# The first image's 3x3 convolution by transformed tiles of two rows by four columns

## The chip, the core and the metric

The kernel runs on one core of a Trainium2 chip. The metric is the device time of one execution in microseconds (us), given as the median of a few runs. TensorE (PE in the profile) multiplies matrices and loads its weights in a second stream (PEld); VectorE (DVE), ScalarE (ACT) and GpSimd (POOL) work elementwise; SyncE (SP) only issues DMAs. Each engine has its own instruction queue and works through it in order; semaphores connect them.

## What is computed

Two images of 256 channels and 64x64 pixels go through two layers, each of them a group normalisation, a block and a residual sum. Layer 0 is attention over all 4096 pixels with eight heads. Layer 1 has two branches. The attention branch works twice on blocks of 64 pixels; the convolution branch makes 576 channels from the same q, k and v and runs a grouped 3x3 convolution over them:

```python
x = x + _L0_conv_ref(_gn(x), ...)
x = x + _L1_conv_ref(_gn(x), ...)

# in layer 1
q, k, v = (_c1x1(x, w, b) for the three weights)
ctx = _sa(blockify(fq), blockify(fk), blockify(v), oh, ow)         # attention over a grid
feats = ...(_bn_relu(_c1x1(ctx, lr_W_w), ...))
ctx2 = _sa(qx, kx, vx, DH, DW)                                     # attention in a block
out_att = ...(_bn_relu(_c1x1(ctx2, sr_W_w), ...))
f_all = jnp.einsum('bidn,oi->bodn', jnp.concatenate([qh, kh, vh], 1), fc_w)
out_conv = lax.conv_general_dilated(f_conv, dep_w, (1, 1), ((1, 1), (1, 1)),
                                    feature_group_count=hd, ...)
return rate1 * out_att + rate2 * out_conv
```

All of it is float32. The kernel multiplies the 1x1 weights into the grouped weights, so that the convolution branch is one dense 3x3 convolution from 256 channels of the normalised x to 256 channels, plus a bias that differs at the image's edges.

## The kernel before

An image is cut into eight tiles of 512 pixels (8 rows), with the channels in two halves of 128 partitions. The images follow one another, and for each come four stages: `project0` (q, k and v of layer 0), `attention0`, `layer1_first` (the grid attention, which leaves `feats`) and `layer1_second` (the block attention and the convolution, tile by tile, and the output). While the first image ends, the generator `following()` fetches the second image's x, takes its statistics and normalises it; `step()` in the last two tiles of `layer1_second` moves it on.

In one tile t of `layer1_second`, TensorE makes the hidden and final q and k (`branch`), then in `group_attention` the values (`pvs`), the scores (`sp`), the transposes (`at`) and the context (`pc`); VectorE does the softmax between scores and transposes, and copies the transposed blocks (`bd`). The convolution is cut into steps, one step at each of up to three `spots` of a tile: spot 0 between the q and the k branch, spot 1 behind the scores, spot 2 behind the context.

The convolution is done on transformed tiles. The first image uses tiles of two rows by two columns (`conv_transform`, `conv_step`): the image falls into four strips of 16 rows, and each strip has four steps, one for each column term, 16 in all. The second image uses tiles of two rows by four columns (`wide_transform`, `wide_step`): two strips of 32 rows, six column terms, 12 steps. A step of either kind has 16 products, each of 128 by 128 by 256, and each of these is two instructions in float32. So a step has 32 matmuls. It consists of

- the transform of the normalised image `xp`: GpSimd takes a difference or sum of columns (`col`); in the wide kind VectorE adds a second term, one instruction per channel half (L1158), and a third (L1161); then GpSimd makes the four row terms `v`. `conv` asks for the transform of the next step before the products of this one;
- the products into one PSUM tile `mm`, of which there is only one, so that the next step's products wait until all of it has been read;
- a copy by ScalarE and four additions by VectorE that read `mm` and leave two output rows `z`;
- additions of `z` into the x tiles. In the wide kind z counts for up to four column phases with factors `BY`: 16 instructions of 128x256 for the column terms 1 to 4, four for the terms 0 and 5 (L1212).

The weights of the first image are made by `conv_weights` on VectorE, written to memory as 16 blocks, fetched by `fetch_conv_weights` (L1013), transposed by TensorE (L1022), scaled, and written back to `wf_kept`. The second image's `WideWeights` has four places in on-chip memory for its six sets. It fetches four of them, makes one new set (number 4) into `wf_more` and one in place (number 3) with GpSimd in `widen`, and exchanges sets between steps as `NEXT` says. The wide kind needs the image's columns apart by phase, so in the second image the x tiles are copied into that order by VectorE at the end of `layer1_first` (L1488).

The order on the engines comes from a planner that works with estimated costs, except inside `tc.manual_schedule`, where the named engines keep the order of the program. In `layer1_second` that is TensorE always, and VectorE too for the second image and for the last two tiles of the first. `tc.issue_after(i)` queues what is in it behind instruction i on that instruction's engine. Buffers: x tiles and some results share nine (`xpool`), short-lived tiles share twelve (`w4`), a transform's `col` has one. When a convolution's strip is complete, `give` adds the x tile to the attention's result and writes it out, which frees the x tile for the second image's load. `conv_edges` adds the edge terms on ScalarE.

Of the kernel before, what the change touches and what calls it, by code (L numbers as in the profile page):

```python
# [10 lines left out]
F32 = mybir.dt.float32  # L11
# [3 lines left out]
ALU = mybir.AluOpType  # L15
# [26 lines left out]
def direct_layers(ctx: ExitStack, tc: tile.TileContext, a: dict, out: bass.AP, bad: bass.AP):  # L42
# [966 lines left out]
    def fetch_conv_weights(b):  # L1009

        wf = vpool.tile([P, KC, UW, C], F32, tag="vw", name=f"wf_{b}")
        for r in range(4):
            nc.sync.dma_start(out=wf[:, :, 4 * r : 4 * r + 4, :], in_=wf_kept[:, :, 4 * r : 4 * r + 4, :])  # L1013
        if b > 0:
            return wf
        for pos in range(UW):
            r, q = divmod(pos, 4)
            pw = bank([P, KC, C], f"pw_{pos}")
            for k in range(KC):
                for m in range(2):  # L1020
                    block = slice(m * P, (m + 1) * P)
                    nc.tensor.transpose(pw[:, k, block], wf[:, k, pos, block], ident)  # L1022
            scale = (0.5 if r in (1, 2) else 1.0) * (0.5 if q in (1, 2) else 1.0)
            if pos % 2:
                nc.scalar.activation(wf[:, :, pos, :], pw, AF.Copy, scale=scale)
            else:
                nc.vector.tensor_scalar(wf[:, :, pos, :], pw, scale, None, ALU.mult)
        nc.sync.dma_start(out=wf_kept, in_=wf)
        return wf

# [3 lines left out]
    def conv_transform(b, xp, s, q):  # L1037

        def cols(d):
            return xp[:, :, 16 * s : 16 * s + 18, d : d + W - 1 : 2]  # L1040

        def rows(d):
            return col[:, :, d : d + 15 : 2, :]

        terms = ((0, 2, False), (1, 2, True), (2, 1, False), (1, 3, False))
        col = cpool.tile([P, KC, 18, W // 2], F32, tag="col", name=f"col_{b}_{s}_{q}")
        one, two, plus = terms[q]
        (nc.gpsimd.tensor_add if plus else nc.gpsimd.tensor_sub)(col, cols(one), cols(two))
        v = [w4([P, 2, KC, STRIP], f"v_{b}_{s}_{q}_{n}") for n in range(2)]
        for r, (one, two, plus) in enumerate(terms):  # L1050
            dst = v[r // 2][:, r % 2].rearrange("p k (i j) -> p k i j", j=W // 2)
            (nc.gpsimd.tensor_add if plus else nc.gpsimd.tensor_sub)(dst, rows(one), rows(two))  # L1052
        return v

    def conv_step(b, xts, wf, v, s, q, pacc, behind_products=None):


        mm = pacc.tile([P, 2, 4, STRIP], F32, tag="acc", name=f"mm_{b}_{s}_{q}")
        for r in range(4):
            for m in range(2):  # L1060
                for k in range(KC):
                    nc.tensor.matmul(  # L1062
                        mm[:, m, r, :], wf[:, k, 4 * r + q, m * P : (m + 1) * P], v[r // 2][:, r % 2, k, :],
                        start=k == 0, stop=k == KC - 1,
                    )
        if behind_products:
            behind_products()
        z = w4([P, 2, 2, STRIP], f"z_{b}_{s}_{q}")
        nc.scalar.copy(z[:, 1], mm[:, :, 1, :])
        nc.vector.tensor_add(z[:, 0], z[:, 1], mm[:, :, 0, :])  # L1070
        nc.vector.tensor_add(z[:, 0], z[:, 0], mm[:, :, 2, :])
        nc.vector.tensor_sub(z[:, 1], z[:, 1], mm[:, :, 2, :])
        nc.vector.tensor_sub(z[:, 1], z[:, 1], mm[:, :, 3, :])  # L1073
        yield
        bias = kept["bias"][1]
        for half in range(2):
            xs = xts[2 * s + half].rearrange("p m (i r j c) -> p m i r j c", i=4, r=2, c=2)
            for r in range(2):
                zs = z[:, r, :, half * (STRIP // 2) : (half + 1) * (STRIP // 2)].rearrange(
                    "p m (i j) -> p m i j", i=4  # L1080
                )
                for c in range(2):
                    dst = xs[:, :, :, r, :, c]
                    if q - c == 0:
                        for m in range(2):
                            nc.vector.scalar_tensor_tensor(  # L1086
                                dst[:, m], zs[:, m], bias[:, m, 0:1], dst[:, m], ALU.add, ALU.add
                            )
                    elif (q, c) in ((1, 0), (2, 0)):
                        nc.vector.tensor_add(dst, dst, zs)  # L1090
                    elif (q, c) in ((2, 1), (3, 1)):
                        nc.vector.tensor_sub(dst, dst, zs)

    NQ, NC, WIDE = 6, 4, W // 4
    wf_more = dram.tile([P, KC, 4, C], F32, name="wf_more")

    class WideWeights:

        TURNS = [(0, q) for q in range(NQ)] + [(1, q) for q in reversed(range(NQ))]
        NEXT = {(0, 0): 4, (0, 1): 5, (1, 5): 1, (1, 4): 0}  # L1100

        def __init__(self, b):
            self.wf = vpool.tile([P, 4, KC, 4, C], F32, tag="vw", name=f"wf_{b}")
            for q in (0, 5, 1, 2):
                self.fetch(q, 3 if q == 5 else q)

        def of(self, q):
            return self.wf[:, q % 4]

        def fetch(self, q, place):  # L1110
            for k in range(KC):
                if q == 4:
                    src = wf_more[:, k]
                else:
                    src = wf_kept[:, k].rearrange("p (r q) c -> p r q c", q=4)[:, :, min(q, 3), :]
                nc.sync.dma_start(out=self.wf[:, place, k], in_=src)

        def widen(self, r):

            stage = w4([P, 2, T], f"wide_{r}")  # L1120
            fourth, tmp = (stage[:, n, :].rearrange("p (k c) -> p k c", k=KC) for n in range(2))
            w = [self.wf[:, q, :, r, :] for q in range(4)]
            nc.gpsimd.tensor_sub(tmp, w[1], w[2])
            nc.gpsimd.tensor_scalar(tmp, tmp, 2.0, None, ALU.mult)
            nc.gpsimd.tensor_scalar(w[3], w[3], 4.0, None, ALU.mult)
            nc.gpsimd.tensor_add(w[3], w[3], w[0])
            nc.gpsimd.tensor_sub(fourth, w[3], tmp)
            nc.gpsimd.tensor_add(w[3], w[3], tmp)
            nc.sync.dma_start(out=wf_more[:, :, r, :], in_=fourth)

        def used(self, s, q):
            if (s, q) in self.NEXT:
                new = self.NEXT[s, q]
                self.fetch(new, new % 4)
# [7 lines left out]
    def wide_transform(b, xp, s, q):  # L1142
# [18 lines left out]
        nc.vector.tensor_add(col, col, cols(fourth))  # L1161
# [207 lines left out]
    def layer1_first(b, put, check, st, groups):  # L1369
# [79 lines left out]
        with tc.manual_schedule(engines={E.PE}):  # L1449

            before = None
            for t in range(NT + 1):
# [28 lines left out]
                if b and 2 <= t < 6:  # L1481
                    kept["wide"].widen(t - 2)
                if b and t:
                    new = xpool.tile([P, KC, T], F32, tag="x", name=f"xphase_{t - 1}")
                    old = st.xts[t - 1].rearrange("p k (a j c) -> p k a c j", j=WIDE, c=NC)
                    with tc.issue_after(kept["bd"].ins):
# [833 lines left out]
```

## Time and profile before

| | us |
|---|---|
| median of three runs | 2995.36 (2994.68 to 2996.34) |
| the profiled execution | 2997.0 |
| its span, first to last instruction | 2995.2 |
| TensorE, VectorE, ScalarE, GpSimd busy | 2942.2, 2497.5, 2337.2, 848.9 |
| first image, convolution products | 1307.2 to 1514.5, 512 matmuls |
| second image, convolution products | 2749.4 to 2962, 384 matmuls |

The profile is of one execution. A row of a timeline gives the start, the length, the engine, the line, the operation with output and inputs, and how many instructions are merged in it; in brackets stands the idle time before it and what ended that. A row of a table of windows gives the stretch and its length, then busy time and instructions of TensorE, its weight loads, VectorE, ScalarE and GpSimd, then the granted TensorE clock, the DMA engines' share and GB/s. Tile names show which stage an instruction belongs to: `lr` is `layer1_first`, `sr` is `layer1_second`.

### The profile page before, as it was taken

What the parts mean: (1) busy time and instruction counts of PE and PEld (TensorE: products, weight loads), DVE (VectorE), ACT (ScalarE), POOL (GpSimd) and SP (SyncE); (2) the same over time, 40 slices, a digit from 0 to 9 for tenths busy, and PEclk for the clock granted to TensorE, in tenths of its full rate; (3) what the DMA queues carried; (4) which work ended last, traced back from release to release, by engine and by line L of the source; (5) the groups of instructions that cost most, each with busy time, mean ns of one, the idle gap of its engine ahead of it and who ended that gap; (6) DMA issues with size and microseconds to landing.
All of it is one profiled execution on the core that took longest, in us unless ns stands there. A gap on an engine that the chain in (4) does not pass through costs nothing. (4 is left out here: it accounts for less than half of the span.)

```text
span 2995.2 us, 63912 instructions
## 1 busy us (share of the span) xinstructions
PE 2942.2 (98%) x25043; PEld 1826.5 (61%) x25043; DVE 2497.5 (83%) x3180; ACT 2337.2 (78%) x3283; POOL 848.9 (28%) x934
## 2 busy tenths in 40 slices
PE   7999999999999999999999999999999999999998
PEld 4555556665555556667765565566665555567665
DVE  4598998999899999966655989989998989965874
ACT  2699999999999995543236999999999999954433
POOL 1032222332232222055500222223222222262430
PEclk9999999999999999999999999999999999999999
DMA  7979778897888771131159797788978877730010
GB/s 259 274 142 181 145 162 166 161 184 149 166 178 161 149 166 51 57 138 44 59 178 264 146 180 149 163 165 162 186 147 169 176 157 153 154 91 28 8 57 30
DMA packets 254339, 430.76 MB, mean 144 GB/s; under 512 B 99352, under 2 KB 118604, under 8 KB 251852
## 3 DMA queue, kind: packets, MB, share of 16 engines
q0 software_dynamic: 96960, 237.57, 41.4%
q1 hardware_dynamic: 156924, 188.76, 23.3%
q8 instruction: 198, 3.24, 0.5%
q14 instruction: 113, 0.93, 0.1%
q10 hardware_dynamic: 144, 0.26, 0.0%
HBM read 124.27 MB, written 69.44 MB: 65 GB/s over the span
## 5 line engine op out<-in xcount | busy, mean ns | idle before, releaser
L600 ACT ACTIVATE es<-ring 128x512 f32<-128x512 f32 (+2 forms) x1574 | 1201.7, 904 | 37.6 <-PE ring L594 23.3
L594 PE MATMUL ring<-q,k 128*128 128x512 f32 x4096 | 1085.5, 407 | 7.8 <-ACT es L600 5.7
L646 DVE TENSOR_TENSOR e<-e,es 128x1024 f32<-128x1024 f32 (+1 forms) x942 | 1029.7, 1155 | 29.6 <-ACT es L600 28.1
L594 PEld LDWEIGHTS ring<-q,k 128*128 128x128 f32 x4096 | 730.9, 188 | 384.6 <-ACT es L600 117.5
L600 ACT ACTIVATE v<-ring 128x512 f32<-128x512 f32 (+2 forms) x1036 | 784.9, 891 | 17.2 <-PE ring L594 8.8
L609 PE MATMUL av<-es,v 128*32 128x256 f32 (+1 forms) x9648 | 722.6, 389 | 0.0
L646 DVE TENSOR_TENSOR e<-e,v 128x1024 f32<-128x1024 f32 (+1 forms) x624 | 669.3, 1130 | 16.8 <-ACT v L600 16.0
L609 PE MATMUL av<-v 128*32 128x256 f32 x6224 | 506.0, 389 | 0.0
L609 PEld LDWEIGHTS av<-es,v 128*32 128x32 f32 x9648 | 325.1, 109 | 263.9 <-issue 105.0
L609 PEld LDWEIGHTS av<-v 128*32 128x32 f32 x6224 | 222.2, 109 | 170.3 <-issue 70.8
L656 POOL DMA_DIRECT2D es<-es x116 | 99.0, 853 | 436.5 <-ACT es L600 406.5
L656 POOL DMA_DIRECT2D acc<-es x126 | 126.2, 1007 | 129.8 <-ACT es L600 38.8
L654 POOL DMA_DIRECT2D es<-es x20 | 11.4, 568 | 492.4 <-ACT es L600 263.3
L656 POOL DMA_DIRECT2D es<-v x74 | 63.3, 855 | 292.1 <-ACT v L600 256.5
L656 POOL DMA_DIRECT2D v<-es x114 | 115.8, 1016 | 24.7 <-ACT es L600 9.3
L1062 PE MATMUL mm<-v,wf 128*128 128x256 f32 x512 | 113.6, 380 | 0.9 <-DVE z L1073 0.9
L656 POOL DMA_DIRECT2D acc<-v x86 | 88.8, 1032 | 88.7 <-DMA acc<-es 36.6
L1062 PEld LDWEIGHTS mm<-v,wf 128*128 128x128 f32 x512 | 96.4, 190 | 16.1 <-issue 3.4
L1052 POOL TENSOR_TENSOR v<-col 128x512 f32<-128x512 f32 x64 | 83.0, 1325 | 74.2 <-DVE x L1086 23.1
L1166 POOL TENSOR_TENSOR v<-col 128x512 f32<-128x512 f32 x48 | 60.5, 1290 | 113.3 <-DVE col L1161 105.3
L1181 PE MATMUL mm<-v,wf 128*128 128x256 f32 x384 | 85.6, 381 | 0.0
L984 DVE SCALAR_TENSOR_TENSOR prep<-prep 128x256 f32<-128x256 f32 x198 | 83.7, 478 | 0.4
(283 smaller groups left out, 2818.7 us busy)
## 6 DMA issues: line engine op xcount, KB each, us to landing
acc<-es POOLq DMA_DIRECT2D x122, 512.0 KB, 6.2
acc<-v POOLq DMA_DIRECT2D x78, 512.0 KB, 6.2
es<-es POOLq DMA_DIRECT2D x136, 256.0 KB, 4.1
v<-es POOLq DMA_DIRECT2D x134, 256.0 KB, 5.2
k<-wk_halves SPq DMA_DIRECT2D x64, 512.0 KB
q<-wq_halves SPq DMA_DIRECT2D x256, 128.0 KB
v<-v POOLq DMA_DIRECT2D x88, 256.0 KB, 4.9
es<-v POOLq DMA_DIRECT2D x86, 256.0 KB, 4.2
```

The lines of the kernel that those rows point to most:

```text
L594: touch(nc.tensor.matmul(sc[:, i, :], held["k", g // 2][:, j * P : (j + 1) * P], held["q", g, u // 2][:, u % 2, :], start=True, stop=True, ...
L600: nc.scalar.activation(dst, sc, AF.Exp, scale=SC0), set(range(at % BANKS, at % BANKS + m))
L609: note(nc.tensor.matmul(dst[HD0 * u : HD0 * u + HD0, n], lhs, rhs(u)[:, n], start=start, stop=stop))
L646: nc.vector.tensor_add(dst[:, s, :], dst[:, s, :], src)
L654: nc.gpsimd.dma_start(out=dst, in_=src)
L656: nc.gpsimd.dma_start(out=dst, in_=src, accum_op=ALU.add)
L984: nc.vector.scalar_tensor_tensor(acc, src, s, acc, ALU.mult, ALU.add)
L1052: (nc.gpsimd.tensor_add if plus else nc.gpsimd.tensor_sub)(dst, rows(one), rows(two))
L1062: nc.tensor.matmul(mm[:, m, r, :], wf[:, k, 4 * r + q, m * P : (m + 1) * P], v[r // 2][:, r % 2, k, :], start=k == 0, stop=k == KC - 1,)
L1166: (nc.gpsimd.tensor_add if plus else nc.gpsimd.tensor_sub)(dst, rows(one), rows(two))
L1181: nc.tensor.matmul(mm[:, r, :, m, :], wide.of(q)[:, k, r, m * P : (m + 1) * P], v[r // 2][:, r % 2, k, :], start=k == 0, stop=k == KC - 1,)
```

## The change

The first image's convolution uses the wide kind too, and the old kind is dropped.

- Steps: 12 instead of 16, three in each of tiles 2, 3 and 4, two in tile 5, one in tile 6. The column terms run 0, 1, 2, 5, 3, 4 in the first strip and 4, 3, 2, 5, 1, 0 in the second. The sum that is L1161 in the second image is done by GpSimd in the first.
- Weights: `fetch_conv_weights` stores the transposed weights as four sets in four places. Sets 0, 1, 2 and 5 are used first; then `widen`, called after the third and the fourth step for two rows each, makes sets 3 and 4 in the places of 0 and 1 (one GpSimd and three VectorE instructions for each row), and writes both to `wf_more`. Sets 1 and 0 are fetched again in the second strip. The second image fetches all six and makes none.
- x tiles: ScalarE copies the first image's tiles into phase order in `layer1_first`, behind the `feats` activations.
- Output: the factor `rate1` moves from `give` to a ScalarE instruction behind the activation of each half; `give` becomes a sum in phase order. The tiles 0 to 3 are handed out behind tile 3, the tiles 4 and 5 at the end of tile 6.
- Order: VectorE keeps program order from tile 2 on. Tiles 5 and 6 go into the image one tile earlier, tile 7 too.
- Second image: `following()` first loads five x tiles instead of seven, and the other two in a step of its own; no convolution step stands in tile 7 any more, and `step()` is called in other places.

```diff
     class WideWeights:
...
         def __init__(self, b):
+            if b == 0:
+                self.turns = [(0, q) for q in (0, 1, 2, 5, 3, 4)] + [(1, q) for q in (4, 3, 2, 5, 1, 0)]
+                self.places = {0: 0, 1: 1, 2: 2, 5: 3, 3: 0, 4: 1}
+                self.next = {(1, 4): 1, (1, 3): 0}
+                self.made = 0
+            else:
+                self.turns = [(0, q) for q in range(NQ)] + [(1, q) for q in reversed(range(NQ))]
+                self.places = {q: q % 4 for q in range(NQ)}
+                self.next = {(0, 0): 4, (0, 1): 5, (1, 5): 1, (1, 4): 0}
...
+        def widen(self, n):
+
+            for r in range(self.made, self.made + n):
+                w = [self.wf[:, place, :, r, :] for place in range(4)]
+                nc.gpsimd.tensor_sub(w[1], w[1], w[2])
+                nc.vector.scalar_tensor_tensor(w[0], w[3], 4.0, w[0], ALU.mult, ALU.add)
+                nc.vector.scalar_tensor_tensor(w[0], w[1], 2.0, w[0], ALU.mult, ALU.add)
+                nc.vector.scalar_tensor_tensor(w[1], w[1], -4.0, w[0], ALU.mult, ALU.add)
+            self.made += n
+            if self.made == 4:
+                for place in range(2):
+                    for k in range(KC):
+                        nc.sync.dma_start(out=wf_more[:, place, k], in_=self.wf[:, place, k])
...
-        nc.vector.tensor_add(col, col, cols(fourth))
+        (nc.vector if b else nc.gpsimd).tensor_add(col, col, cols(fourth))
...
-                if b and 2 <= t < 6:
-                    kept["wide"].widen(t - 2)
-                if b and t:
-                    new = xpool.tile([P, KC, T], F32, tag="x", name=f"xphase_{t - 1}")
+                    kept["wide"].load(b)
+                if t:
+                    new = xpool.tile([P, KC, T], F32, tag="x", name=f"xphase_{b}_{t - 1}")
                     old = st.xts[t - 1].rearrange("p k (a j c) -> p k a c j", j=WIDE, c=NC)
-                    with tc.issue_after(kept["bd"].ins):
+                    with tc.issue_after(kept["bd" if b else "feats"].ins):
                         for k in range(KC):
-                            nc.vector.tensor_copy(phases(new)[:, k], old[:, k])
+                            (nc.vector.tensor_copy if b else nc.scalar.copy)(phases(new)[:, k], old[:, k])
...
-        spots = {t: (0, 1, 2) for t in range(2, 7)} | {7: (0,)} if b == 0 else {
+        spots = {2: (0, 1, 2), 3: (0, 1, 2), 4: (0, 1, 2), 5: (0, 1), 6: (0,)} if b == 0 else {
             0: (1, 2), 1: (0, 1), 2: (0, 1), 3: (0, 1), 4: (0, 1), 5: (1,), 6: (1,)
         }
-        images = {1: range(5), 3: (5, 6), 4: (7,)} if b == 0 else {1: (5, 6), 2: (7,)}
+        images = {1: range(5), 2: (5, 6), 3: (7,)} if b == 0 else {1: (5, 6), 2: (7,)}
...
             done += 1
+            if b == 0 and done in (3, 4):
+                wide.widen(2)
...
-            with tc.manual_schedule(engines={E.PE, E.DVE} if near or b else {E.PE}):
+            with tc.manual_schedule(engines={E.PE, E.DVE} if b or t > 1 else {E.PE}):
...
+                    if b == 0:
+                        nc.scalar.activation(res[:, m, :], res[:, m, :], AF.Identity, scale=wts["rate1"])
...
-                    conv(step)
+                    conv()
+                if near and not seam:
+                    for n in sorted(results):
+                        give(n)
+                    step(2)
...
-            for n in sorted(n for n in results if done >= (NQ * (n // 4 + 1) if b else 4 * (n // 2 + 1))):
+            for n in sorted(n for n in results if done >= NQ * (n // 4 + 1)):
                 give(n)
...
-        xts = ahead["xts"] = load_x(1, range(NT - 1))
+        xts = ahead["xts"] = load_x(1, range(NT - 3))
...
+        yield
+        xts += load_x(1, range(NT - 3, NT - 1))
         yield
         xn = ahead["xn"] = apool.tile([P, KC, N], F32, tag="A", name="xn_1")
```

## The prediction

> **What bounds the kernel now.** First the page's first part and its slices: TensorE is busy for 2942.2 of 2995.2 us and its clock is full almost everywhere, so time is won only where TensorE's own work gets less and nothing else takes its place. Then the windows, one per tile of the stage that the change touches: three tiles of the first image (three convolution steps each), and the second image's heaviest tile, which already runs the new kind of step, though only twice per tile.
>
> ```profile
> PE 2942.2 (98%) x25043; PEld 1826.5 (61%) x25043; DVE 2497.5 (83%) x3180; ACT 2337.2 (78%) x3283; POOL 848.9 (28%) x934
> ```
> ```profile
> 1342.70:1383.90 41.20, 41.20 (x196) 30.26 (x195) 25.58 (x46) 13.28 (x20) 21.98 (x15) 1.00 0.15 52
> 1383.90:1425.10 41.20, 41.20 (x196) 30.26 (x195) 24.66 (x47) 12.49 (x23) 23.56 (x16) 1.00 0.15 50
> 1425.10:1466.30 41.20, 41.20 (x196) 30.26 (x195) 23.17 (x45) 12.15 (x21) 21.61 (x15) 1.00 0.01 3
> 2773.95:2811.57 37.62, 34.79 (x163) 24.01 (x162) 36.57 (x71) 16.63 (x34) 14.87 (x10) 1.00 0.00 0
> ```
>
> Columns: length, then TensorE, weight loads, VectorE, ScalarE, GpSimd, clock, DMA. In the first image TensorE never waits and VectorE has some 16 us to spare per tile. In the last row TensorE lost 2.83 us and VectorE is busy for 97%, with only two steps in the tile. The timeline of VectorE and GpSimd says why:
>
> ```profile
> 2784.50 9.41 DVE L1212 SCALAR_TENSOR_TENSOR xphase<-z,xphase 128x256 f32<-128x256 f32 x16
> ...
> 2822.07 5.46 DVE L1212 SCALAR_TENSOR_TENSOR xphase<-z,xphase 128x256 f32<-128x256 f32 x16
> ```
> ```profile
> 2784.24 2.69 POOL L1166 TENSOR_TENSOR v<-col 128x512 f32<-128x512 f32 x2
> 2787.02 2.25 POOL L1156 TENSOR_TENSOR col<-xp 128x1088 f32<-128x1088 f32 x1
> ```
>
> The same 16 additions take 5.46 us alone and 9.41 us when GpSimd works beside them: VectorE all but stands while GpSimd's instruction runs.
>
> **Removed: four steps.** A step is 32 matmuls at 0.22 us, 7.07 us in the timeline; 16 steps become 12: **-28.3 us** on the saturated engine. The 64 weight transposes stay. If nothing else bound, the span would be 2966.9.
>
> **Added on VectorE and GpSimd, tiles 2 to 4** (nine of the twelve steps, three per tile, each tile 41.2 us of TensorE: 123.6). VectorE now works in program order there. One step with 16 additions (seven of the nine: all but columns 0 and 5) costs VectorE two column terms 1.35 (L1158 in the second image), four readings of the products 2.74 (L1202 to L1205), and the additions. GpSimd's share is 2.19 for the differences, 2.2 for the sum that moves to it (not in the trace; between VectorE's 1.29 for it and L1156's 2.19 for the same shape, taken at the latter, the same engine), and 5.0 for four row terms: 9.4 us, of which about three row terms and the next step's differences, 5.9, fall on the additions. Here **a rule speaks against the change**: the Trainium skill, "SBUF - State Buffer", section "SBUF: two separate sides", says that VectorE with two SBUF inputs and GpSimd exclude each other for whole instructions. By the rule the pair above would take 5.46 + 4.77 of GpSimd (2784.50 to 2789.27) = 10.2; the row says 9.41, so some 0.27 us per GpSimd instruction still overlaps. By the rule the additions cost 5.46 + 5.9 = 11.4, by the row 10.3. I take the row: 14.4 per heavy step. A light step (4 additions) is 1.35 + 2.74 + 1.4 + about 2.1 blocked = 7.6.
>
> Sum for VectorE: 7 x 14.4 = 100.8; 2 x 7.6 = 15.2; three softmaxes with the block copies and the wait for the exponential, 3.7 each, 11.1; the made sets 12 instructions of 128x512, 0.7 each by the rate of L1563 when undisturbed (737 ns), 8.4; the eight output additions of tiles 0 to 3, all handed out behind tile 3, at 0.95 (L1561: 5.66 us for six), 7.6. Total 143.1, or 151 by the rule, against 123.6: **19.5 us too much**, 27 by the rule. VectorE can run late by a few microseconds only, since the next product waits for the last reading of the one PSUM tile and the next transform is queued behind the additions. Following the queues in program order with these durations, TensorE waits about 11 us at step 4 (the first made set: its last two rows wait behind step 3's additions and two GpSimd differences that stand behind the row terms), 6 at step 7 and 6 at tile 4's softmax (the output additions are ahead of both), and 5 elsewhere: 28. I take **+25**, near the walk because the order is fixed. Bounds: 0 if VectorE's lateness were absorbed, 33 by the rule.
>
> **The clock.** The windows around TensorE's one long gap before the change:
>
> ```profile
> 1236.00:1238.00 2.00, 0.38 (x3) 0.41 (x4) 1.95 (x6) 0.06 (x1) 0.00 (x0) 1.00 0.00 0
> 1238.00:1240.00 2.00, 2.00 (x12) 2.00 (x12) 2.00 (x6) 0.64 (x1) 0.00 (x0) 0.50 0.00 0
> ```
>
> A wait of 2.73 us was followed by about 3 us at half clock, some 1.5 us lost; the 2.80 us wait at 2809.75 was followed by none. The Trainium skill, "TensorE: Matmul & The Clock Gate", part 1, wants a whole idle window of about 3.4 us that runs free; by it none of my waits need cost anything below that, and the longer ones up to 1.7 us each. With four of 4 us or more I take two hits: **+3** (0 to 7).
>
> **The seam to the second image.** Before, its statistics were aggregated at 1502.7 and TensorE took them at 1514.38, 11.7 us to spare, because steps 13 to 16 stood in tiles 6 and 7. Now tile 6 has one step, tile 7 none, and the last two x tiles are loaded only after the outputs of tiles 4 and 5 are added, at the end of tile 6. Counted from tile 7's start on TensorE: block copy done at -2.2, four additions at 0.95 to +1.6, two 512 KB loads about 4.5 (issue 0.9, then 1 MB at about 370 GB/s, and a start; an estimate from the earlier loads), two tiles' last statistics 1.4, aggregation 0.6: +8.1. TensorE is there at +4.5, since 2.7 us of the next projection fill tile 6's softmax: **+4** (1 to 7). From there on the order is as before.
>
> **The smaller parts.** The weights' load now has 1 KB pieces: the old one ran at 378 GB/s between 1294 and 1305, the second image's load in such pieces at 351 between 2640 and 2650; TensorE waits for it row by row, **+1**. ScalarE's edge terms wait for the later additions with the next tile's activations behind them (the 2.80 us wait above is that): **+2** (0 to 4). Its 16 column-phase copies, some 0.8 us each, are queued behind the feature activations of layer1_first, where ScalarE idled for about 2 us before each exponential; the scaling by rate1, two per tile, meets an engine at 30%: both at 0, and up to 3 if a copy falls ahead of the exponential. The second image loses the making of its fourth set on GpSimd, about 35 us of work under a TensorE that is busy 25 of 25 us there: 0. Write-backs of weights are as large as before and not waited for.
>
> Sum: -28.3 + 25 + 3 + 4 + 1 + 2 = +6.7 on a span of 2995.2; the profiled run took 2997.0, the median of runs, 2995.36, is next to the span, so **3002 us**.
>
> **Rivals.** (A, 0.50) As summed: VectorE and GpSimd take back all or more; 2996 to 3015. (B, 0.25) They take back only part, since lateness runs out into tile 5 with its two steps: the floor of 19.5 less 5 of tile 4's last additions, no clock loss, 7 for the rest: -28.3 + 14.5 + 7 = -6.8, 2988; 2983 to 2996. (C, 0.20, the other side) TensorE stays the bound: GpSimd and VectorE hardly meet, and only seam and load cost, -28.3 + 5 = 2972. For it: the second image's other tiles, 34.93 of 35.28 and 34.29 of 34.29 us busy. Against: these have at most one heavy step each where the lock bites, and 41.2 us for three. It decides where VectorE's queue stays under 41 us per tile, that is additions below 9 us. (D, 0.05) The made sets arrive much later, by the writes that read them or full buffers: above 3015.
>
> **How the numbers follow.** Within 0.2% (6 us, about what a measurement of this kernel tells from no change) is 2989.4 to 3001.4. Faster: C, and somewhat over half of B (0.14): 0.34. Same: the rest of B (0.11) and a third of A (0.17): 0.28. Slower: two thirds of A (0.33) and D: 0.38. Leaving out half of C and the top of A and D gives the range 2973 to 3013; A's own is 2996 to 3015.
>
> **What would show it.** Right: windows of tiles 2 to 4 of 45 to 55 us with VectorE above 90% and TensorE below; L1212's mean over 0.6 us in the first image (0.46 busy before); waits of products for the row terms and of the transposes for the softmax; half-clock slices. Wrong: TensorE at full in those tiles, or a stage some 28 us shorter; a seam without a wait for the statistics.

## The result, and the profile after

The changed kernel takes **3021.75 us** (median of 4 runs, 3018.94 to 3023.53) against 2995.02 (2990.25 to 2996.34) for the kernel before on the same chip: a ratio of **1.0091** (95% interval 1.0074 to 1.0109), 26.7 us slower. The prediction, 3002, had the sign and not the size; 3021.75 lies above its range. The profiled execution's span is 3021.7 us, 26.5 more than before.

The page's first part, the changed kernel:

```profile
PE 2932.9 (97%) x24915; PEld 1812.0 (60%) x24915; DVE 2554.5 (85%) x3217; ACT 2359.9 (78%) x3313; POOL 826.0 (27%) x906
```

TensorE has 128 matmuls fewer, the four steps. Yet its busy time fell by 9.3 us and not by 28.3, so 19.0 us of matmul time came back at half clock, and its idle time rose from 53.0 to 88.8. -28.3 + 19.0 + 35.8 is the 26.5. Where this happened is read from the windows, cut at TensorE's first matmul of steps 1, 4, 7 and 10 and of the second image's query projection (length, TensorE, weight loads, VectorE, ScalarE, GpSimd, clock, DMA):

```profile
1307.35:1347.06 39.71, 34.53 (x181) 27.04 (x179) 30.02 (x47) 11.59 (x18) 28.60 (x19) 1.00 0.32 106
1347.06:1400.73 53.67, 45.82 (x194) 32.15 (x194) 52.52 (x75) 13.34 (x22) 32.39 (x19) 0.94 0.10 40
1400.73:1457.39 56.66, 46.52 (x194) 33.25 (x194) 55.72 (x81) 11.47 (x20) 30.87 (x19) 0.91 0.35 121
1457.39:1564.06 106.67, 96.70 (x411) 61.01 (x412) 72.92 (x131) 43.80 (x79) 29.21 (x20) 0.94 0.21 69
```

Tiles 3 and 4, the second and third row, take 53.7 and 56.7 us where they took 41.2. VectorE is busy for 98% of both, TensorE for 85% and 82% of them at a clock of 0.94 and 0.91. The same cuts in the profiled runs (e12 has its steps in other places), each from the start times in TensorE's timeline:

| kernel | step 1 to step 10 | step 10 to second image's queries | the rest |
|---|---|---|---|
| before | 117.9 | 117.1 (88.8 without four steps) | 1453.0 |
| after | 150.0 | 106.7 | 1457.6 |
| e1 awake | 150.1 | 106.0 | 1456.3 |
| e2 no additions | 142.6 | 102.7 | 1456.5 |
| e3 one row term | 127.8 | 100.6 | 1455.0 |
| e4 third sum on VectorE | 143.7 | 102.9 | 1458.9 |
| e5 narrow additions | 127.2 | 102.7 | 1455.7 |
| e6 narrow sets | 139.7 | 104.9 | 1460.6 |
| e7 seam | 150.0 | 102.8 | 1459.8 |
| e8 pairs and sum | 134.1 | 102.0 | 1457.2 |
| e9 all on VectorE | 147.7 | 101.7 | 1454.2 |
| e10 rearranged | 134.2 | 95.3 | 1451.8 |
| e11 outputs one by one | 130.5 | 100.2 | 1455.6 |

So the 26.5 us are +0.1 ahead of step 1 (1307.23 to 1307.35), **+32.2** from step 1 to step 10, -28.3 + **17.9** from there to the second image's projections, and +4.6 in the rest, whose value goes from 1451.8 to 1460.6 over the runs, nearly all of which leave that part as it is.

VectorE and GpSimd at step 3, and the same additions at step 11, the changed kernel's timelines of the two engines:

```profile
1341.99 1.34 DVE L1109 SCALAR_TENSOR_TENSOR col<-col,xp 128x544 f32<-128x544 f32 x2
1343.26 0.67 DVE L1153 TENSOR_TENSOR z<-z,mm 128x512 f32<-128x512 f32 x1
...
1345.29 0.69 DVE L1156 TENSOR_TENSOR z<-z,mm 128x512 f32<-128x512 f32 x1
1346.01 11.55 DVE L1163 SCALAR_TENSOR_TENSOR xphase<-z,xphase 128x256 f32<-128x256 f32 x16
1357.49 0.68 DVE L1074 SCALAR_TENSOR_TENSOR wf<-wf 128x512 f32<-128x512 f32 x1
...
1491.73 5.45 DVE L1163 SCALAR_TENSOR_TENSOR xphase<-z,xphase 128x256 f32<-128x256 f32 x16
```
```profile
1343.48 2.16 POOL L1112 TENSOR_TENSOR col<-col,xp 128x1088 f32<-128x1088 f32 x1 [6.72 <-DVE col L1109]
1345.72 5.56 POOL L1117 TENSOR_TENSOR v<-col 128x512 f32<-128x512 f32 x4
1351.36 2.24 POOL L1107 TENSOR_TENSOR col<-xp 128x1088 f32<-128x1088 f32 x1
```

The 16 additions take 11.55 us beside GpSimd and 5.45 without it. GpSimd is busy for 7.50 us of these 11.55: nearly all of the four row terms (L1117) and the whole next difference (L1107) fall on the additions. Its third sum (L1112) stands ahead, beside the readings of the products, which do not slow down (0.67 to 0.69 us each). One row term and the addition beside it, from the same two timelines:

```profile
1346.96 1.47 POOL L1117 TENSOR_TENSOR v<-col 128x512 f32<-128x512 f32 x1
1347.21 1.50 DVE L1163 SCALAR_TENSOR_TENSOR xphase<-z,xphase 128x256 f32<-128x256 f32 x1
```

Each of GpSimd's five instructions holds one addition for about its own length (the difference holds one for 2.39 us); the other eleven take 0.41 us each, as they do alone.

What TensorE waited for, the changed kernel's timeline of TensorE (in brackets the wait and what ended it):

```profile
1347.06 8.86 PE L1132 MATMUL mm<-v,wf 128*128 128x256 f32 x32 [4.45 <-POOL v L1117]
...
1368.69 5.17 PE L1132 MATMUL mm<-v,wf 128*128 128x256 f32 x16 [3.10 <-DVE z L1156]
...
1400.73 7.17 PE L1132 MATMUL mm<-v,wf 128*128 128x256 f32 x32 [2.91 <-POOL v L1117]
...
1423.92 10.01 PE L1132 MATMUL mm<-v,wf 128*128 128x256 f32 x32 [4.78 <-POOL v L1117]
...
1436.53 0.69 PE L1262 MATMUL at_sr<-ident,e_sr 128*128 128x128 f32 x2 [2.59 <-DVE e_sr L1257]
...
1494.75 3.57 PE L1548 MATMUL prq_sr<-hq_sr,wt_fq 128*128 128x512 f32 x4 [4.52 <-ACT hq_sr L1295]
...
1517.46 0.44 PE L1262 MATMUL at_sr<-ident,e_sr 128*128 128x128 f32 x2 [2.56 <-DVE e_sr L1257]
...
1521.88 3.65 PE L1282 MATMUL pc_sr<-bd,vs_sr 128*128 128x128 f32 x16 [1.23 <-DVE bd L1271]
...
1534.04 0.38 PE L360 MATMUL pm_l<-mv_l,group 128*128 128x2 f32 x2 [1.65 <-DVE mv_l L345]
```

As foretold, the row terms, the readings and the softmax are late. Behind most of these waits the matmuls run slowly: a step takes 10.01 us at 1423.92 instead of 7.07.

### The profile page after: what moved, and what is told of

Read it like the earlier page. It is cut to its first block, busy times and chain, and to the rows that moved or that the text cites. A ratio compares the mean times of both kernels' runs of the same rounds, so it can differ in the third digit from the quotient of the medians.

```text
span 3021.7 us, 63689 instructions
## 1 busy us (share of the span) xinstructions
PE 2932.9 (97%) x24915; PEld 1812.0 (60%) x24915; DVE 2554.5 (85%) x3217; ACT 2359.9 (78%) x3313; POOL 826.0 (27%) x906
## 5 line engine op out<-in xcount | busy, mean ns | idle before, releaser
L646 DVE TENSOR_TENSOR e<-e,es 128x1024 f32<-128x1024 f32 (+1 forms) x942 | 1029.3, 1154 | 28.0 <-ACT es L600 26.5
L646 DVE TENSOR_TENSOR e<-e,v 128x1024 f32<-128x1024 f32 (+1 forms) x624 | 669.3, 1129 | 18.1 <-ACT v L600 17.4
L1132 PE MATMUL mm<-v,wf 128*128 128x256 f32 x768 | 177.7, 391 | 18.2 <-POOL v L1117 13.9
L1132 PEld LDWEIGHTS mm<-v,wf 128*128 128x128 f32 x768 | 148.8, 196 | 46.1 <-POOL v L1117 20.0
L1163 DVE SCALAR_TENSOR_TENSOR xphase<-z,xphase 128x256 f32<-128x256 f32 x288 | 164.4, 641 | 0.7
L1117 POOL TENSOR_TENSOR v<-col 128x512 f32<-128x512 f32 x96 | 126.1, 1345 | 115.8 <-DVE col L1112 106.9
L654 POOL DMA_DIRECT2D es<-es x20 | 11.4, 568 | 500.8 <-ACT es L600 250.3
L656 POOL DMA_DIRECT2D v<-es x114 | 115.6, 1014 | 26.1 <-ACT es L600 10.3
L656 POOL DMA_DIRECT2D v<-v x76 | 78.6, 1034 | 13.8 <-ACT v L600 5.8
```

The costliest lines, as they stand in the source:

```text
L646: nc.vector.tensor_add(dst[:, s, :], dst[:, s, :], src)
L654: nc.gpsimd.dma_start(out=dst, in_=src)
L656: nc.gpsimd.dma_start(out=dst, in_=src, accum_op=ALU.add)
L1132: nc.tensor.matmul(mm[:, r, :, m, :], wide.of(q)[:, k, r, m * P : (m + 1) * P], v[r // 2][:, r % 2, k, :], start=k == 0, stop=k == KC - 1,)
L1163: kept["added"] = nc.vector.scalar_tensor_tensor(xs[:, :, c, :], zs, by, xs[:, :, c, :], ALU.mult, ALU.add)
```

## The experiments

"Theory V" is what the first four runs left standing: VectorE's queue, in its fixed order and in turns with GpSimd, sets the time from step 3 on. The ratio is to the kernel before, run beside each.

**e1: TensorE kept awake.** Dummy matmuls, of an identity by itself into a spare bank, fill eight waits: ahead of four steps, as below, and in the same manner ahead of softmaxes' transposes, the block copy and tile 6's projection. `awake` issues so many of them.

```
+    AWAKE = {(0, 5): 24, (0, 3): 14, (1, 4): 12, (1, 3): 24}
...
+        if b == 0 and (s, q) in AWAKE:
+            awake(f"{s}_{q}", AWAKE[s, q])
         for r in range(4):
             for m in range(2):
```

> Eight places of the first image where TensorE waits (ahead of steps 4, 5, 7 and 8, of tile 1's and of tiles 4's and 6's softmax, and inside tile 6's q projection) are filled with 12 to 24 matmuls of 128x128 that compute nothing, 134 in all, some 16 us that fit into the waits. Theory 1 (the half clock that follows the waits is lost on the path): the half-clock stretches at these places vanish, some 13 us come back, about 3009 us (3005 to 3012). Theory 2 (VectorE, held up by GpSimd, is what the first image's tiles 2 to 4 take their time from; TensorE's slow stretches lie inside that): the clock is full, the waits grow by as much, 3017 to 3022 us. Theory 3 (the low clock has nothing to do with the waits): the same slices stay at half clock, 3020 us or more.

3020.14 us, ratio 1.0089 (1.0072 to 1.0106): as the changed kernel. The windows from step 1 to step 10, first of the changed kernel, then of e1:

```profile
1307.35:1457.39 150.04, 126.87 (x568) 92.43 (x566) 138.26 (x201) 36.41 (x60) 91.86 (x55) 0.94 0.25 88
```
```profile
1304.56:1454.64 150.08, 139.92 (x741) 107.72 (x739) 138.29 (x201) 36.30 (x60) 91.97 (x55) 0.99 0.25 88
```

The clock goes from 0.94 to 0.99, and the stretch takes 150.08 us instead of 150.04. That is theory 2: TensorE's slow matmuls lie inside VectorE's lateness; made fast, they only wait longer. Step 1 begins 2.8 us earlier, behind tile 1's filled wait.

**e2: no additions.**

```
-                if by:
+                if by and b:
```

> The first image's 144 additions of the convolution's products into x are left out, so its output lacks the convolution; all else is as in the changed kernel. Theory 2: VectorE has some 95 us less to do, TensorE is full in tiles 2 to 6, only the seam (about 3 us) and the load are left: 2967 to 2976 us. Rival (the made sets and the output additions in VectorE's fixed order hold it up, whatever the additions take): waits at steps 4 and 7 stay, 2985 us or more.

3010.9 us, ratio 1.0058 (1.0041 to 1.0074). The number and the waits at steps 4 and 7 (9.79 and 6.16 us) are the rival's, but not for its reason, and the run does not tell the two apart: both waits end on GpSimd's work. The next transform is queued behind the last addition; with none, the order of the queues became another. In its trace VectorE began to read step 3's products at 1351.02, 12 us after ScalarE's copy of them, behind column terms that waited 7.12 us for a difference of GpSimd. e5 asks the same question with the order kept.

**e3: one row term of four.**

```
+            if r and b == 0:
+                break
             dst = v[r // 2][:, r % 2].rearrange("p k (i j) -> p k i j", j=WIDE)
...
-                        ... v[r // 2][:, r % 2, k, :],
+                        ... v[r // 2 * (b > 0)][:, r % 2 * (b > 0), k, :],
```

> In the first image GpSimd makes one of the four row terms of a step, and the products of all four rows read it, so the convolution's result is another; VectorE's and TensorE's instructions are the same in number and shape. Theory 2 [...]: the 16 additions fall from about 0.64 us each towards 0.34, VectorE stays under 41 us per tile, 2968 to 2982 us. Rival (VectorE's own work in its fixed order is too long without GpSimd): additions stay above 0.55 us each, 3000 us or more.

2991.34 us, ratio 0.9989 (0.998 to 0.9998): 30 us less, between the two numbers expected. The additions in the groups of VectorE, first image, of the changed kernel and of e3 (busy us, mean ns):

```profile
L1163 DVE SCALAR_TENSOR_TENSOR xphase<-z,xphase 128x256 f32<-128x256 f32 x144 | 97.9, 750 | 0.3
```
```profile
L1165 DVE SCALAR_TENSOR_TENSOR xphase<-z,xphase 128x256 f32<-128x256 f32 x144 | 72.5, 575 | 0.3
```

33 row terms less on GpSimd, some 45 us by their mean of 1.37, take 25.4 us off VectorE's additions. The gain is smaller than foretold, since 72.5 us is still well above the 49 that they take alone (e9): GpSimd's remaining row term and its difference still fall on them.

**e4: the third sum back on VectorE.**

```
-        (nc.vector if b else nc.gpsimd).tensor_add(col, col, cols(fourth))
+        nc.vector.tensor_add(col, col, cols(fourth))
```

> The third column sum of the first image is given back to VectorE, as in the second image: 1.29 us more on VectorE and 2.2 less on GpSimd per step. Theory 2 with exclusion of whole instructions: the sum of both engines' time falls by 0.9 per step, the time falls by 2 to 8 us, 3014 to 3020. Rival (VectorE's amount of work alone decides): 9 x 1.29 us more, 3030 us.

3014.17 us, ratio 1.0066 (1.0049 to 1.0082), as theory 2 has it. VectorE's groups of e4:

```profile
L1163 DVE SCALAR_TENSOR_TENSOR xphase<-z,xphase 128x256 f32<-128x256 f32 x144 | 84.8, 660 | 0.3
...
L1112 DVE TENSOR_TENSOR col<-col,xp 128x1088 f32<-128x1088 f32 x11 | 14.2, 1290 | 0.3
```

VectorE takes over 14.2 us of sums, and its additions get 13.1 us shorter (97.9 to 84.8): with the sum on VectorE, row terms begin beside the readings (at step 3 at 1344.27, the readings at 1344.11), and less of them falls on the additions. So this part of the change, meant to relieve VectorE, relieved it of nothing.

**e5: additions one column wide**, in the same order.

```
-                        xs[:, :, c, :], zs, by, xs[:, :, c, :], ALU.mult, ALU.add
+                        *[w if b else w[:, :, 0:1] for w in (xs[:, :, c, :], zs)], by,
+                        xs[:, :, c, 0 : WIDE if b else 1], ALU.mult, ALU.add
```

> The first image's 144 additions into x take one column in sixteen, so most of the convolution is missing from its output; they stay where they were in VectorE's order, and GpSimd's and TensorE's orders are the same as in the changed kernel. Theory V (from step 3 to tile 5's softmax VectorE never stands still, and its queue sets the stage): additions fall from 98 us to about 15, TensorE is full in tiles 2 to 5, what is left is the seam: 2974 to 2988 us. Rival O (the fixed order and the chain GpSimd, VectorE, GpSimd of a transform set it, whatever VectorE's amount): waits for row terms of 3 us and more stay, above 2995 us.

2995.37 us, ratio 0.9997 (0.9988 to 1.0006): 26 us less than the changed kernel by the medians, 28 by the ratios, and no less than the kernel before. The time is rival O's, but not its sign: no step waits more than 1.88 us for row terms, and VectorE is busy for 102.8 of the 105.0 us from step 3 to step 10. Theory V's number failed on the additions' 15 us: they took 62.4. VectorE's and GpSimd's timelines of e5 at step 3, and at step 11 beside a GpSimd without work:

```profile
1339.93 7.92 DVE L1163 SCALAR_TENSOR_TENSOR xphase<-z,xphase 128x16 f32<-128x16 f32 x16
...
1463.29 1.64 DVE L1163 SCALAR_TENSOR_TENSOR xphase<-z,xphase 128x16 f32<-128x16 f32 x16
```
```profile
1339.66 5.00 POOL L1117 TENSOR_TENSOR v<-col 128x512 f32<-128x512 f32 x4
1344.74 2.19 POOL L1107 TENSOR_TENSOR col<-xp 128x1088 f32<-128x1088 f32 x1
```

Sixteen additions of 16 numbers a partition each, 1.64 us of work, take 7.92 us, which ends 0.9 us after GpSimd's row terms and difference (1346.93). What VectorE has to add is 3.81 us less than in the changed kernel (1.64 for 5.45), and the additions end up 3.63 us shorter. The time that it stands beside GpSimd hardly depends on their size: 6.28 us here, 6.10 there.

**e6: narrow sets.**

```
-                w = [self.wf[:, place, :, r, :] for place in range(4)]
+                w = [self.wf[:, place, :, r, 0:4] for place in range(4)]
```

> The 16 instructions that make the first image's two other sets take 4 of 256 columns, so the sets are wrong; order and count are as in the changed kernel. Theory V: VectorE has some 10 us less to do in a stretch in which it never stands still, so the time falls by 8 to 11 us: 3011 to 3014. Rival (the making hides beside TensorE): 3018 us or more.

3013.6 us, ratio 1.0056 (1.0039 to 1.0072); step 1 to step 10 falls by 10.3 us. Four of the 16 instructions are GpSimd's, so its work shrinks too. On VectorE the sets go from 11.4 to 4.3 us (one still takes 2.55), the first image's additions from 97.9 to 94.6, its column terms from 17.4 to 16.3: 11.5 us less, paid nearly in full.

**e7: the seam.**

```
+        with tc.issue_after(kept["added"].ins):
             for k in range(KC):
                 st.tile(k, NT - 1)
...
                     conv()
+                    if near:
+                        for n in sorted(results):
+                            give(n)
```

> The statistics of the second image's last tile are queued behind step 12's additions instead of in front of step 11's readings, and the outputs of tiles 4 to 5 are added right behind step 12 instead of behind tile 6. If the waits of tiles 6 and 7 (4.52 for tile 6's activation, 1.23 for the block copy, 1.65 for the statistics) and their half clock are a loss of their own: 5 to 9 us less, 3013 to 3017. If they only stand for VectorE's lateness: 3020 us.

3018.28 us, ratio 1.007 (1.0054 to 1.0087), between the two numbers: 3.5 us by the medians, some 6 by the ratios, 3.9 in the table's second column. The waits for the statistics and the block copy went (0.74 for another copy stayed). The long one, for tile 6's activation, stayed at 4.69. The changed kernel's timelines show what this wait is, ScalarE first, then VectorE:

```profile
1487.24 0.77 ACT L1295 ACTIVATE hq_sr<-phq_sr,vecs 128x512 f32<-128x512 f32 x1
...
1493.53 0.51 ACT L1172 ACTIVATE xphase<-xphase,edges 128x8 f32<-128x8 f32 x2 [4.91 <-DVE xphase L1163]
1493.94 0.76 ACT L1295 ACTIVATE hq_sr<-phq_sr,vecs 128x512 f32<-128x512 f32 x1
```
```profile
1482.77 0.69 DVE L1153 TENSOR_TENSOR z<-z,mm 128x512 f32<-128x512 f32 x1
1488.62 0.69 DVE L341 BATCH_NORM_STATS2 stats_l<-xn 128x6 f32<-128x512 f32 x1 [5.17 <-DMA xn<-in_x_dram]
...
1491.73 5.45 DVE L1163 SCALAR_TENSOR_TENSOR xphase<-z,xphase 128x256 f32<-128x256 f32 x16
```

ScalarE's second activation for tile 6 (1493.94) stands behind an edge term that waits for step 11's additions, and VectorE had put its readings behind a load of the second image's last tile (5.17 us of idle). e7 takes the load out of the way; the additions then begin 6.2 us earlier, counted from step 10, beside GpSimd, take 9.08 us instead of 5.45, and TensorE is no further: step 12 begins 42.1 us after step 10, in the changed kernel 40.8.

**e8: additions in pairs, the third sum on VectorE.** s = z1 + z2 and d = z1 - z2 first, so that each of the four columns gets one addition for two steps (even columns from s, odd ones from d, by the signs in `by_q`).

```
+            nc.vector.tensor_sub(z, z_first, z)
+            nc.vector.scalar_tensor_tensor(z_first, z_first, 2.0, z, ALU.mult, ALU.subtract)
...
-            for c, by in enumerate(BY[q]):
+            for c, by in enumerate(by_q):
```

> Both images add the columns 1 and 2, and 3 and 4, of a transformed tile into x in pairs (sum and difference first, 18 units of additions per tile become 14); the first image's last six steps have the order 4, 3, 5, 2, 1, 0; its third column sum is VectorE's again. Theory V: VectorE loses 11 to 16 us in the first image, the sum's move another 7.6, the second image's two waits for activations behind additions go (3 to 5): 2993 to 3003 us. Rival (the additions come in larger bursts, and one more buffer is held): 3008 us or more.

3002.7 us, ratio 1.002 (1.0013 to 1.0027), at the upper end of theory V. Step 1 to step 10 falls by 9.6 us below e4's. The second image gained nothing: its additions in one burst made a step wait 5.15 us for its row terms.

**e9: the first image's transforms wholly on VectorE.**

```
+        eng = nc.gpsimd if b else nc.vector
-        (nc.gpsimd.tensor_add if plus else nc.gpsimd.tensor_sub)(col, cols(one), cols(two))
+        (eng.tensor_add if plus else eng.tensor_sub)(col, cols(one), cols(two))
```

and so for the third sum and the row terms.

> In the first image VectorE makes the whole transforms of the columns and rows itself; GpSimd does only the sets' differences there. A step gives VectorE four row terms at some 0.69 us, a difference and a sum at 1.29: 5.3 us more, 59 us over eleven transforms. Theory V (the two engines take turns, so GpSimd's 9.4 us of a step are paid by VectorE anyway): its 16 additions go back to 5.46 us, the sum of a step with 16 additions stays within 1 us, one with 4 gets 2 to 3 longer: 3014 to 3026 us. Rival (GpSimd works beside VectorE, and the additions are slow for another reason): VectorE has 59 us more to do, 3050 us or more.

3018.65 us, ratio 1.0076 (1.0061 to 1.0092). VectorE's groups of e9:

```profile
L1164 DVE SCALAR_TENSOR_TENSOR xphase<-z,xphase 128x256 f32<-128x256 f32 x144 | 49.2, 416 | 0.3
L1118 DVE TENSOR_TENSOR v<-col 128x512 f32<-128x512 f32 x44 | 27.5, 686 | 0.3
...
L1108 DVE TENSOR_TENSOR col<-xp 128x1088 f32<-128x1088 f32 x11 | 15.2, 1381 | 0.0
L1113 DVE TENSOR_TENSOR col<-col,xp 128x1088 f32<-128x1088 f32 x11 | 15.2, 1378 | 0.3
```

VectorE does 57.9 us more (27.5 + 15.2 + 15.2), its additions shrink from 97.9 to 49.2 us, and the kernel is no slower for it. GpSimd's help with the transforms had been worth nothing.

**e10: rearranged**, several edits at once: e8's pairs for the first image, e4's sum, e7's seam; and the first transform behind tile 1's block copy instead of ahead of it, one of the weight sets' four rows made earlier, two steps of the first image's second strip exchanged (5 ahead of 2, as in e8), two outputs at most after tile 3, and tile 7's query product in tile 6's softmax:

```
+                if b == 0 and t == 2:
+                    ahead[0] = wide_transform(b, xp, *turns[0])
...
-            if b == 0 and done in (3, 4):
-                wide.widen(2)
+            if b == 0 and done in (2, 3, 4):
+                wide.widen(2 if done == 4 else 1)
...
-            for n in sorted(n for n in results if done >= NQ * (n // 4 + 1)):
+            for n in sorted(n for n in results if done >= NQ * (n // 4 + 1))[: 2 if b == 0 and t == 3 else None]:
...
+                    carried = {"q": hidden("fq1", V_FQ1, "q", f_next, f"sr_{b}_{t + 1}")}
```

> Six edits of the first image together: additions of columns 1 and 2, 3 and 4 in pairs, the third column sum on VectorE, the first transform behind tile 1's block copy, the sets made in three parts (one row of four behind step 2, one behind 3, two behind 4), the outputs of tiles 0 to 3 in two parts, the seam's order of e7 with tile 7's first projection pulled into tile 6's softmax. From e8's profile (3003 us) less its waits with the half clock behind them: tile 1's copy 3, step 5 4, step 8 6, tile 6's softmax 3.5, the seam 5, the second image's unpaired again 4. Theory V: 2978 us (2970 to 2988), faster than the kernel before. Rival (VectorE's lateness only moves the waits): 2992 us or more.

2991.56 us, ratio **0.9988** (0.9982 to 0.9995): faster than both kernels, by 3.5 us over the one before, and short of its range. The seam did most of what was asked (95.3 in the second column, 6.7 below e8, for the 8.5 expected); step 1 to step 10 did not move from e8's 134.

**e11 and e12** go after e10's two longest waits. e11 makes the first row's outputs one by one, one behind each of steps 7 to 10 (`if b == 0 and done > NQ and min(results) < 4: give(min(results))`), and issues the second image's first six statistics later in tile 6, behind the block copy; e12 does so too, makes one more of the weight sets' rows a step earlier, and moves one step from tile 3 to tile 5 (`3: (1, 2), 4: (0, 1, 2), 5: (0, 1, 2)`).

> As e10, but the outputs of tiles 0 to 3 are added one behind each of steps 7 to 10, and in tile 6 the block copy stands before the second image's statistics. e10's profile has 4.19 us of waiting at step 8 for VectorE with three outputs ahead of its readings, 2.6 lost at half clock behind it, and 1.39 for the block copy. Theory V: these go, 2984 us (2979 to 2989). Rival (lateness moves on): as e10, 2991.

> As e11, with tile 3 given two steps and tile 5 three (the others as they were), and the sets made one row behind step 2, two behind step 3, one behind step 4. e10 waits 3.28 us within step 5 for the sets and loses 2.7 at half clock, while VectorE stands idle for 17 us in tiles 4 and 5. Theory V: these 6 us go too, 2978 us (2973 to 2984). Rival (one more result is held and the last steps are denser, so tile 6 is late): 2988 us or more.

2994.44 us, ratio 0.9992 (0.9983 to 1.0), and 2996.36 us, ratio 0.9999 (0.9991 to 1.0007). Both miss. In e11 step 8 no longer waits, but step 10 waits 3.51 us for its row terms, and the statistics come 4.87 us late at the seam. In e12 the wait for the sets is gone, and tile 3's activation waits 5.82 us, step 6 4.59. The rival, that lateness moves on, is right for these two.

## Why the prediction failed

The forecast for the span was +6.7 us, and +26.5 came. Of the 19.8 between them, 4.2 lie between step 1 and step 10 (32.2 for the 25 and the clock's 3), 11.9 behind that (17.9 for seam and edge terms, 6) and 4.6 in the second image (for 0); ahead of step 1 it was 0.9 less than forecast (0.1 for 1).

**The mechanism of tiles 2 to 4 was right.** Excess of VectorE in turns with GpSimd, tiles 3 and 4 above 50 us, waits for row terms and softmax: all of it is in the profile. e9 shows that the turns cause it, since the transforms cost the same time on VectorE, and e3 that less work on GpSimd takes the time back.

**VectorE and GpSimd, +25: the step that failed first.** Taken from the trace, the work that was summed to 143.1 us is 153.1, which is 29.5 more than the 123.6: readings 24.7, column terms 13.3 (12.2 was summed), additions of steps 1 to 9 86.3 (79.1), sets 11.4 (8.4), outputs 7.5, softmaxes with block copies 9.9 (11.1). The wrong term is the amount of GpSimd's work beside the additions, "about three row terms and the next step's differences, 5.9". It is 7.0 to 8.0 at the steps with 16 additions: nearly all of the four row terms, and the difference. The cause lies within the change, the third sum moved to GpSimd: it fills the time of the readings, in which row terms cost VectorE nothing, and pushes them under the additions (e4: 13.1 us). The choice of the row over the rule was right: at step 3 (11.55 - 5.45) / 7.50 = 0.81 us of standing per us of GpSimd, as 0.83 in the row used; whole instructions after the rule of the Trainium skill, "SBUF - State Buffer", section "SBUF: two separate sides", would make it 13.0. The single rows above agree with the rule that one engine waits for a whole instruction of the other; what the sum by the rule leaves out is that about one addition gets through for each instruction of GpSimd. That is 0.28 us for each of the five here, where an addition takes 0.34 alone, and 0.13 in e5, where it takes 0.10; so e5's 6.28 us of standing for 6.92 of GpSimd is nearer to the rule. The rule's 11.4 for a step came out near only because its amount was too small as well. Measured from step 1 to step 10: +32.2 for 25.

**The clock, +3.** Nine waits, not the two that were taken, were followed by half clock, 19 us in the sum; but to add these, or 3, is wrong in kind for step 1 to step 10. There another engine sets the time, and a slow TensorE costs nothing (e1: 150.08 for 150.04).

**Seam +4, edge terms +2: the step with the larger miss.** Tile 5 and what follows lost 17.9 us: 10.0 idle (106.67 less 96.70) and 7.9 at half clock (96.70 less 88.8). The idle time is four waits. Tile 6's activation (4.52) is the edge terms' +2: the right mechanism at less than half its price. The softmax of tile 6, which no step covers any longer and which the prediction had taken as filled by the next projection, cost 2.56, and the statistics 1.65: together the seam's +4, in another place. The block copy, behind six statistics (1.23), was in no term, and half clock behind these waits only in the +3.

VectorE's lateness at the end of tile 4 explains little of it. Step 10 still waits 1.48 us for its row terms, but step 11's readings begin only 0.5 us behind ScalarE's copy of the products (1482.77, the copy ends at 1482.28); then VectorE stands 5.17 us for the load that e7 moves away. In e3, where tile 6's activation waits 0.39 us, the same stretch takes 100.6, still 11.8 more than 88.8: 6.8 idle, mostly at the softmax (2.56), the block copy (0.80) and the statistics (3.06), and 5.0 at half clock. So most of the loss comes, as far as the runs show, with what the change took out of tiles 6 and 7. e10, which fills tile 6's softmax with tile 7's projection, has no wait there. How the rest divides between waits and clock stays open: in e1 two of the waits are filled, the statistics are then waited for 3.64 us, and the stretch takes 106.0.

**The weights' load, +1**, and the smaller parts: step 1 begins 0.1 us later than before, but not as reasoned. The load made nobody wait; instead tile 1's block copy stood behind the first transform's column terms, 3.29 us of waiting on TensorE, in the place of the waits for the load.

**The second image, 0.** +4.6 in this execution: the wait of 2.79 us at 2832.49, which was there before, was this time followed by half clock (1.7 us; the last section shows why), and 10.0 us instead of 7.9 passed after the last matmul. Nothing in the runs ties these to the change.

**The rivals.** B was right that the lateness runs out into tile 5, and wrong in its numbers: 32.2 us up to there for 14.5, and 17.9 behind it for some 7. C needed additions below 9 us; they took 11.1 to 11.8. D has the right side of 3015, but the sets, 11.4 us of VectorE's queue, are a share of A's mechanism and not a late arrival.

**Open:** what would be won with all four parts (pairs, sum, sets, seam) balanced. e10 still has TensorE waiting in tiles 3 and 4, though VectorE is busy for only 43.5 of 50.0 and 42.6 of 48.6 us there, so that the order of its queue counts as well as its amount.

## What to carry to other kernels

When two engines take turns, add their times before you move work between them, and ask beside which instructions the moved work will run: GpSimd's sums cost VectorE nothing beside the readings of PSUM (0.67 to 0.69 us each with and without them), and row terms cost it some four fifths of their length beside additions from SBUF. Where an engine other than TensorE sets the pace, TensorE's clock and single waits are no longer terms of a sum. And when work moves out of a stage's last tiles, list the waits that it covered there, and what covers each of them now.

## What the runs showed of the hardware that was not expected

- Each GpSimd instruction held one addition for about its own length, whatever the addition's size: 16 additions of 16 numbers a partition took 7.92 us (1.64 alone), 16 of 256 took 11.55 (5.45 alone), beside five GpSimd instructions each.
- Transforms taken from GpSimd and given to VectorE, 57.9 us of work there, left the kernel's time as it was (1.0076 for 1.0091).
- Half clock followed waits well under the idle window of about 3.4 us that the Trainium skill, "TensorE: Matmul & The Clock Gate", part 1, gives: after 2.59, 2.56 and 1.65 us in the changed kernel (the matmuls at 1436.53, 1517.46 and 1534.04), while 2.91 us at 1400.73 was followed by none. What decides is mostly where a wait falls. In the changed kernel's trace the stretches at half clock last 3.41 or 6.83 us (but for one behind the last instruction) and begin whole multiples of 3.41 us apart. Windows on this grid, two around the wait of 2.91 us and two around that of 2.79 in the second image:

```profile
1395.58:1399.00 3.42, 2.24 (x6) 0.70 (x4) 3.35 (x6) 1.55 (x2) 2.42 (x1) 1.00 0.01 2
1399.00:1402.41 3.41, 1.68 (x8) 1.50 (x9) 3.38 (x5) 0.00 (x0) 3.33 (x4) 1.00 0.00 0
2829.18:2832.59 3.41, 0.62 (x3) 0.10 (x1) 3.41 (x11) 1.82 (x6) 0.09 (x1) 1.00 0.00 0
2832.59:2836.01 3.42, 3.42 (x5) 1.34 (x6) 3.39 (x8) 2.04 (x3) 0.00 (x0) 0.50 0.00 0
```

  The first wait is split over two windows, idle for 1.18 and 1.73 us; the second falls into one, idle for 2.79. The same wait before the change (2809.75) was split, 1.18 and 1.61. Between 1250 and 2980 us, all eight windows idle for 2.41 us or more were followed by half clock, and of the seven idle for 1.5 to 1.9 us one, that of 1.65. What decides in such windows no run here shows.
